# Layer 1 of a two-layer GNN with expert FFN: the expert mask moved to VectorE, the block's beginning divided

## The chip, the core and the metric

The kernel runs on one core of a Trainium2 chip. The core has five engines with their own instruction queues: TensorE (PE; its weight loads are shown apart, as PEld), VectorE (DVE), ScalarE (ACT), GpSimd (POOL) and SyncE (SP). Each engine takes its instructions in order, and an instruction waits for others by semaphores. The metric is the device time of one execution in microseconds; less is better.

## What is computed

Two layers, each a graph aggregation and then a feed-forward part, over 6250 nodes with 256 features and 100,000 edges sorted by destination. In layer 1, with which the change deals:

```python
# aggregation
h = layernorm(x) @ weight
x = x + segment_sum(edge_weight[:, None] * h[src], dst) + bias
# feed-forward part: one of 32 experts for each node
xf = layernorm(x)
idx = argmax(xf @ router_w.T + router_b, axis=-1)
h = relu(einsum('nd,ndh->nh', xf, W1[idx]) + b1[idx])          # 64 hidden values
out = relu(einsum('nh,nhd->nd', h, W2[idx]) + b2[idx])
x = x + out
```

## The kernel before

**Tiles and blocks.** The nodes are 49 tiles of 128 rows; `X` holds all of them in SBUF. The feed-forward parts work on blocks of up to 4 tiles (`NB`). `blocks1` (L360) cuts layer 1 into 13 blocks: 3 tiles, eleven times 4, and 2.

**Every expert for every node.** Layer 1 computes the hidden values of all 32 experts, 32 x 64 = 2048, in 16 chunks of 128 (`NC1`), two experts a chunk. In `hidden1` two float32 products (`k` = 0, 1) give a chunk's hidden values for the block in `ph`; a third product adds the mask. `sel[:, c, :]` (bfloat16, made once at L1025) has -2^127 (`FAR`) where a hidden row belongs to an expert, and `cold` is 1 where a node did not choose that expert, so every hidden value of an expert that was not chosen becomes hugely negative, and the ReLU on ScalarE (L989) makes it 0. `outs1` multiplies the chunk `hm` by the second weights into `py` (L1000), which gathers all 16 chunks; `end1` takes the ReLU of it, adds `X` and stores the rows.

**Which expert.** `begin1` normalises a block's rows (`norm_t`: statistics, `xn`, transposes into `nT`), multiplies by the router's weights (`pl`, L957), finds the highest expert on VectorE (L962 to L968), and transposes the one-hot rows (`pg`, L973) into `hotT` and `cold`.

**The aggregation.** `columns1` goes through the edges in columns of 128. For each column `gather` (L201) fetches 128 rows of the normalised features from DRAM by an indirect DMA that GpSimd issues; ScalarE (L230) and VectorE (L231) split the weighted rows into a float32r pair `m`; a one-hot matrix `s` (L222, VectorE, for three columns at once) sends them to their destinations in a matmul (L277) that sums in `acc`. There are 24 buffers for gathered rows, 12 for `m`. When 8 columns are done, a half tile's sums are taken out of `acc`; the steps of `summed` and `by_weight` run 2, 6 and 9 columns later (`LAG - 4`, `LAG - 1`, with `LAG` = 10), and at the last of them the sums of a tile, transposed and multiplied by the weights (L214), are added to `X` (L215). The first 64 columns are done during layer 0; 718 are left for layer 1.

**The order.** The main loop of layer 1 (L1029 to L1049) runs over blocks and chunks. Ahead of each hidden chunk and ahead of each `outs1` it calls `sums.upto`, which emits columns up to a number that `aheads` laid down: spread evenly, so that the sums of the next block are done in time for its `begin1`. That comes after chunk 11 (of 0 to 15) of the block ahead, or after chunk 13 in the first block (L1047), all in one piece. The hidden chunk `c + 1` is emitted ahead of `outs1` of chunk `c`. The compiler may shift instructions a little against this order on each engine.

Of the kernel before, what the change touches and what calls it, by code (L numbers as in the profile page):

```python
# [36 lines left out]
NC1 = NX1 * H1 // P  # L37
DST_PAD = 8192
SJ = 3
LAG = 10  # L40
EARLY = 2
FAR = -2.0 ** 127
SRC_PAD = 8191
NEAR = 576
LN_EPS = 1e-5
# [4 lines left out]
def gnn_ffn_kernel(ctx: ExitStack, tc: tile.TileContext, a, out):  # L50
# [64 lines left out]
    good1 = const.tile([P, 1], F32, name="good1")  # L115
    off = const.tile([P, 1], F32, name="off")

    which_x = const.tile([P, NX1], F32, name="which_x")
    nc.gpsimd.iota(which_x, pattern=[[1, NX1]], base=0, channel_multiplier=-1, allow_small_or_imprecise_dtypes=True)
    order = const.tile([P, NX1], F32, name="order")  # L120
    nc.gpsimd.iota(order, pattern=[[-1, NX1]], base=NX1, channel_multiplier=0, allow_small_or_imprecise_dtypes=True)
    edges_rec, edges_val = a["edges_rec"], a["edges_val"]
# [113 lines left out]
    def columns1(pool, psum, js, h, idx, w, bufs):  # L236


        hots, ahead, parts, few = bufs
        first = js.start == 0  # L240
        ends = []

        def summed(q, acc):

            yield
            if first and (q % 2 or q == 2 * NB):
                s = first_sums[:, q // 2, :]
            else:
                s = pool.tile([P, D], F32, tag="sums", name="sums", bufs=few)
            nc.scalar.activation(s, acc[:, 0, :], AF.Copy)  # L250
            nc.vector.tensor_add(s, s, acc[:, 1, :])
            halves[q] = s
            low, high = slice(0, P // 2), slice(P // 2, P)
            if q % 2:
                nc.vector.tensor_add(s[low], s[low], halves[q - 1][low])
            elif first:
                if 0 < q < 2 * NB:
                    nc.vector.tensor_add(halves[q - 1][high], halves[q - 1][high], s[high])
            else:
                if q == 2 * NB:  # L260
                    nc.vector.tensor_add(s, s, first_sums[:, NB, :])
                nc.vector.tensor_add(halves[q - 1][high], halves[q - 1][high], s[high])
                sT = pool.tile([P, 2, P], F32, tag="sT", name="sT", bufs=2)
                yield
                yield from by_weight(psum, halves[q - 1], sT, q // 2 - 1)

        for j in range(js.start, js.stop + (0 if first else LAG)):
            if j < js.stop:
                q, i = divmod(j + CS // 2, CS)
                opens = i == 0 or j == js.start  # L270
                done = i == CS - 1 or j == js.stop - 1
                if opens:
                    acc = psum.tile([P, 2, D], F32, tag="agg", name="acc", bufs=2)
                if (j - js.start) % SJ == 0:
                    s = one_hots(pool, dl_c, j, hots)
                m = weighted(pool, h, idx[:, j:j + 1], w[:, j:j + 1], ahead, parts)
                nc.tensor.matmul(acc, s[:, (j - js.start) % SJ, :], m, start=opens, stop=done)  # L277
                if done:
                    ends.append((j, summed(q, acc)))
            for at, steps in ends:  # L280
                if j - at in (0, 2, LAG - 4, LAG - 1):
                    next(steps, None)
            yield
        for _, steps in ends:
            for _ in steps:
                pass
        yield
# [69 lines left out]

    ramp = [1, 1, 2, 3] + [NB] * 9 + [3, 3]
    blocks0 = [list(range(sum(ramp[:b]), sum(ramp[:b + 1]))) for b in range(len(ramp))]
    ramp = [3] + [NB] * 11 + [2]  # L360
    blocks1 = [list(range(sum(ramp[:b]), sum(ramp[:b + 1]))) for b in range(len(ramp))]

    class Stream:
# [271 lines left out]
    with tc.tile_pool(name="layer0", bufs=1) as wp, tc.tile_pool(name="outs0", bufs=1, side="right") as wo_pool, \  # L635
# [56 lines left out]
        def aggregate0():  # L692
            for b, tiles in enumerate(blocks0):
                idx, dl, w = edges[b]
                for i, t in enumerate(tiles):
                    acc = psum.tile([P, 2, D], F32, tag="agg", name="acc", bufs=2)
                    for j in range(EW):
                        if j % SJ == 0:
                            s = one_hots(wp, dl[:, i, :], j, 3)
                        m = weighted(wp, h0, idx[:, i, j:j + 1], w[:, i, j:j + 1], 12, 6)  # L700
                        nc.tensor.matmul(acc, s[:, j % SJ, :], m, start=(j == 0), stop=(j == EW - 1))  # L701
                        if j == EW - 1:
                            for half in range(2):
                                nc.vector.tensor_add(X[:, t, :], X[:, t, :], acc[:, half, :])
                        yield

            for _ in columns1(wp, psum, range(NE), h1[:LIM, :], idx_e, w_e, (3, 12, 6, 2)):
                yield
            while True:
                yield  # L710
# [84 lines left out]
        def load1(k, half):  # L795
# [4 lines left out]
            else:  # L800
                cs = slice(half * NC1 // 2, (half + 1) * NC1 // 2)
                x = a["L1_ffn_W2"].rearrange("e h d -> (e h) d").rearrange("(c p) d -> p c d", p=P)
                nc.sync.dma_start(w2f[:, cs, :], x[:, cs, :])


        idx_e = wp.tile([P, NE], I32, name="idx_e")
        w_e = wp.tile([P, NE], F32, name="w_e")

        def early_columns():
            nc.vector.tensor_scalar(w_e, src_c[:, :NE], float(LIM), None, op0=OP.is_lt)  # L810
            nc.vector.tensor_tensor(w_e, w_e, val_c[:, :NE], OP.mult)
            nc.vector.tensor_scalar(idx_e, src_c[:, :NE], float(LIM - 1), None, op0=OP.min)


        n_late = len(late)
# [123 lines left out]

    with tc.tile_pool(name="layer1", bufs=1, reuse_waits="tile") as wp, \  # L940
            tc.tile_pool(name="psum_y1", bufs=1, space=bass.MemoryType.PSUM, reuse_waits="tile") as psum_y:

        sel_x = wp.tile([P, NX1, H1], BF, name="sel")
        sel = sel_x.rearrange("q (c s) i -> q c (s i)", s=2)
        nought = wp.tile([P, 2 * D], BF, name="nought")

        done = []
# [1 line left out]
        def begin1(pool, tiles):  # L949

            n = len(tiles)
            nw = n * P
            nT = norm_t(pool, psum, tiles)
            pl = psum.tile([P, NB, NX1], F32, tag="tr", name="pl", bufs=1)
            for j in range(n):
                for k in range(2):
# [11 lines left out]
            nc.vector.tensor_tensor(g, g, m[:, :, None].to_broadcast([P, n, NX1]), OP.is_equal)  # L968
            hots = work.tile([P, NB, P // NX1, NX1], F32, tag="hots", name="hots", bufs=1)
            nc.scalar.activation(hots[:, :n], g[:, :, None, :].to_broadcast([P, n, P // NX1, NX1]), AF.Copy)  # L970
            pg = psum.tile([P, NB * P], F32, tag="tr", name="pg", bufs=1)
            for j in range(n):
                turned = nc.tensor.transpose(pg[:, j * P:(j + 1) * P], hots[:, j], ident)  # L973
            hotT = pool.tile([P, NB * P], BF, tag="hotT", name="hotT", bufs=2)
            done[:] = [turned, nc.scalar.activation(hotT[:, :nw], pg[:, :nw], AF.Copy)]
            cold = pool.tile([P, NB * P], BF, tag="cold", name="cold", bufs=2)
            done.append(nc.vector.tensor_scalar(cold[:, :nw], pg[:, :nw], 0.5, None, op0=OP.is_lt))
            return nT, hotT, cold, nw

        def hidden1(pool, block, c):  # L980
            nT, _, cold, nw = block
            ph = psum.tile([P, NB * P], F32, tag="mm", name="ph", bufs=3)
            for k in range(2):
                nc.tensor.matmul(ph[:, :nw], w1f[:, k, c * P:(c + 1) * P], nT[:, k, :nw],  # L984
                                 start=(k == 0), stop=False)

            nc.tensor.matmul(ph[:, :nw], sel[:, c, :], cold[:, :nw], start=False, stop=True)  # L987
            hm = pool.tile([P, NB * P], F32, tag="hm", name="hm", bufs=4)
            nc.scalar.activation(hm[:, :nw], ph[:, :nw], AF.Relu, bias=b1[:, c:c + 1])  # L989
            return hm  # L990

        def outs1(block, c, now, py, n):
# [22 lines left out]
        with tc.tile_pool(name="flow1", bufs=1, reuse_waits="tile") as flow:  # L1015

            sums = Stream(columns1(flow, psum, range(NE, NREAL), h1, src_c, val_c, (5, EW + 6, 12, 4)))
            cum = [0] + [min(CS * (2 * tiles[-1] + 2) + CS // 2, NREAL) + LAG - NE for tiles in blocks1[1:]]
            plans = aheads(cum, 2 * NC1, [4] + [8] * (len(blocks1) - 1))
            block = begin1(flow, blocks1[0])  # L1020

            behind = ExitStack()
            for ins in done:
                behind.enter_context(tc.issue_after(ins.ins))
            nc.vector.tensor_scalar(sel_x, which_x[:, :, None].to_broadcast([P, NX1, H1]), 0.0, FAR,  # L1025
                                    op0=OP.is_equal, op1=OP.mult)
            nc.vector.memset(nought, 0.0)
            hm = hidden1(flow, block, 0)
            for b, tiles in enumerate(blocks1):  # L1029
# [3 lines left out]
                mine = block  # L1033
                for c in range(NC1):
                    sums.upto(plans[b][2 * c])
                    now = hm
                    if c + 1 < NC1:
                        hm = hidden1(flow, block, c + 1)
# [4 lines left out]
                    if b == 0 and c == 3:  # L1043
                        behind.close()
                    outs1(mine, c, now, py, n)

                    if c == NC1 - (3 if b == 0 else 5) and not last:  # L1047
                        after = begin1(flow, blocks1[b + 1])
                end1(flow, tiles, py)  # L1049

        with tc.tile_pool(name="slow1", bufs=1) as flow:

            def again():
                for t in range(NT):
                    block = begin1(flow, [t])
# [54 lines left out]
```

## Time and profile before

| what | us |
|---|---|
| median of 3 runs | 2898.83 (2892.92 to 2900.43) |
| profiled execution, its time | 2895.13 |
| its span | 2893.4 |
| layer 1's first gather, last gather (start) | 1828.05, 2772.42 |
| first mask matmul of blocks 1, 5, 10, 11, 12 | 1949.8, 2286.5, 2707.9, 2788.7, 2854.0 |
| last matmul's end | 2885.1 |

In the lists of groups the columns are: line, engine, operation, tiles (out<-in), shapes, count | busy time, mean duration in ns of one | idle time of the engine ahead of them and what ended it. In a list of waits: engine and line <- what it waited for: us in total, times, longest. In a timeline: start, duration, engine, line, operation, tiles, shapes, count, and in brackets the idle time ahead of it and what ended that. The slices of the whole span (40 equal ones; digits are tenths):

```profile
PE   5888848888999999999999998779999999999998
DVE  8999977778768767766566555666666666666630
POOL 4666667777767676766675527677777777777720
```

Layer 1 begins at about slice 26; all three are those of the page.

### The profile page before, as it was taken

The page shows a single profiled execution, that of the slowest core. Times are in us where ns is not written, and L with a number is a line of the kernel's source. Part 1 is how long each engine was busy: PE and PEld are TensorE (multiplying, and loading weights), DVE is VectorE, ACT ScalarE, POOL GpSimd, SP SyncE. Part 2 cuts the span into 40 slices and gives each one's busy share as a digit, 9 for nine tenths or more (in the row PEclk, how much of TensorE's full clock was granted, in tenths as well). Part 3 has the DMA queues.
Part 4 walks back from the last instruction along what each step waited for, and adds up shares of the span by engine and source line. Part 5 has one row for each costly group of instructions (what it writes and reads, how often), then busy time and mean ns, then how long its engine had stood idle before and what let it go on. Part 6 is the DMA issues. An engine that isn't in the chain of part 4 may idle for free.

```text
span 2893.4 us, 37030 instructions
## 1 busy us (share of the span) xinstructions
PE 2677.7 (93%) x10336; PEld 1750.2 (60%) x10336; DVE 2012.4 (70%) x4917; ACT 1626.1 (56%) x3790; POOL 1926.1 (67%) x1932
## 2 busy tenths in 40 slices
PE   5888848888999999999999998779999999999998
PEld 2444427665566666666666665556666666666666
DVE  8999977778768767766566555666666666666630
ACT  6777737655555555555555545455555555555532
POOL 4666667777767676766675527677777777777720
PEclk9999978999999999999999999999999999999999
DMA  4000043333333333333332214333333333333310
GB/s 150 19 19 19 19 141 97 101 100 102 92 99 95 90 101 97 91 100 96 91 102 82 78 39 135 109 108 103 107 108 109 106 108 102 108 106 109 109 44 12
DMA packets 123140, 260.73 MB, mean 90 GB/s; under 512 B 32236, under 2 KB 68904, under 8 KB 122920
## 3 DMA queue, kind: packets, MB, share of 16 engines
q0 software_dynamic: 79872, 218.21, 26.2%
q1 hardware_dynamic: 31672, 32.42, 3.4%
q10 hardware_dynamic: 11376, 7.60, 0.8%
q8 instruction: 85, 1.39, 0.2%
q14 instruction: 135, 1.11, 0.1%
HBM read 238.87 MB, written 19.25 MB: 89 GB/s over the span
## 4 chain that ended last, share of the span: by engine, by line
PE 65%; DVE 17%; DMA 8%; issue 4%; ACT 4%; POOL 1%; ACTq 0%; POOLq 0%; DVEq 0%
PE ph L748 19%; PE py L760 10%; PE py L1000 9%; PE ph L984 9%; PE acc L701 6%; PE acc L277 4%; DMA g<-h,src_c 4%; DMA g<-h,idx 3%; DVE loads L527 3%; DVE to L523 2%; DVE m L231 2%; ACT m L230 2%; PE ph L987 1%; PE ph L214 1%; POOL g L201 1%
## 5 line engine op out<-in xcount | busy, mean ns | idle before, releaser
L201 POOL DMA_INDIRECT g<-h,idx x882 | 903.1, 1024 | 391.8 <-DVE m L231 175.2
L201 POOL DMA_INDIRECT g<-h,src_c x718 | 725.6, 1011 | 227.8 <-issue 104.2
L230 ACT ACTIVATE m<-g,w 128x256 fp32r<-128x256 f32 x882 | 394.7, 500 | 260.0 <-PE acc L701 136.0
L751 ACT ACTIVATE hT<-ph,shift,scale 128x512 f32<-128x512 f32 (+3 forms) x480 | 329.0, 696 | 314.6 <-PE ph L748 313.4
L230 ACT ACTIVATE m<-g,val_c 128x256 fp32r<-128x256 f32 x718 | 349.7, 503 | 273.6 <-PE acc L277 132.2
L231 DVE SCALAR_TENSOR_TENSOR m<-g,val_c,m 128x256 fp32r<-128x256 f32 x718 | 337.1, 483 | 211.2 <-ACT m L230 207.6
L231 DVE SCALAR_TENSOR_TENSOR m<-g,w,m 128x256 fp32r<-128x256 f32 x882 | 397.7, 476 | 42.5 <-ACT m L230 41.4
L748 PE MATMUL ph<-nT,w 128*128 128x512 f32 (+3 forms) x960 | 373.1, 524 | 25.0 <-ACT hT L751 24.8
L760 PE MATMUL py<-wo,hT 128*128 128x256 f32 x1568 | 382.1, 387 | 13.8 <-DVE X L762 10.5
L1000 PE MATMUL py<-w,hm 128*128 128x256 f32 x1568 | 386.7, 385 | 3.1 <-ACT hm L989 3.1
L701 PE MATMUL acc<-m,s 128*128 128x512 f32 x882 | 341.4, 490 | 38.0 <-DVE scale L657 24.7
L984 PE MATMUL ph<-nT,w 128*128 128x512 f32 (+2 forms) x832 | 374.8, 571 | 0.0
L748 PE MATMUL ph<-hT,w 128*128 128x512 f32 (+3 forms) x960 | 368.5, 518 | 0.5 <-ACT hT L751 0.5
L760 PEld LDWEIGHTS py<-wo,hT 128*128 128x128 f32 x1568 | 294.7, 193 | 80.8 <-DVE X L762 26.9
L277 PE MATMUL acc<-m,s 128*128 128x512 f32 x782 | 332.2, 499 | 1.7 <-DVE m L231 1.7
L1000 PEld LDWEIGHTS py<-w,hm 128*128 128x128 f32 x1568 | 292.1, 193 | 52.9 <-ACT hm L989 4.6
L222 DVE TENSOR_TENSOR s<-col,dl 128x384 fp32r<-128x384 f32 x294 | 161.4, 551 | 187.0 <-PE acc L701 184.8
L748 PEld LDWEIGHTS ph<-nT,w 128*128 128x128 f32 x960 | 175.2, 195 | 174.2 <-issue 118.1
L989 ACT ACTIVATE hm<-ph,b 128x512 f32<-128x512 f32 (+2 forms) x208 | 136.8, 659 | 200.0 <-PE ph L987 199.6
L748 PEld LDWEIGHTS ph<-hT,w 128*128 128x128 f32 x960 | 176.2, 193 | 118.9 <-issue 88.3
L701 PEld LDWEIGHTS acc<-m,s 128*128 128x128 f32 x882 | 169.7, 195 | 109.8 <-issue 48.9
L984 PEld LDWEIGHTS ph<-nT,w 128*128 128x128 f32 x832 | 157.2, 191 | 101.5 <-issue 81.1
(248 smaller groups left out, 3359.0 us busy)
## 6 DMA issues: line engine op xcount, KB each, us to landing
g<-h,idx POOLq DMA_INDIRECT x882, 2.8
g<-h,src_c POOLq DMA_INDIRECT x718, 2.8
h<-hs SPq DMA_DIRECT2D x25, 256.0 KB, 2.1
X<-in_x_dram SPq DMA_DIRECT2D x12, 512.0 KB, 8.9
out_dram<-o SPq DMA_DIRECT2D x11, 512.0 KB, 3.4
h<-hs SPq DMA_DIRECT2D x9, 512.0 KB, 3.0
w<-in_L_ffn_W_dram ACTq DMA_DIRECT2D x2, 2048.0 KB, 11.2
wo<-in_L_ffn_Wo_dram ACTq DMA_DIRECT2D x1, 2048.0 KB, 20.0
```

The lines of the kernel that those rows point to most:

```text
L201: nc.gpsimd.indirect_dma_start(out=g, out_offset=None, in_=h, in_offset=bass.IndirectOffsetOnAxis(ap=idx, axis=0))
L222: nc.vector.tensor_tensor(s[:, :n], col[:, None, :].to_broadcast([P, n, P]), dl[:, j:j + n, None].to_broadcast([P, n, P]), OP.is_equal)
L230: nc.scalar.activation(m[:, 0, :], g, AF.Copy, scale=w)
L231: nc.vector.scalar_tensor_tensor(m[:, 1, :], g, w, m[:, 0, :], op0=OP.mult, op1=OP.subtract)
L277: nc.tensor.matmul(acc, s[:, (j - js.start) % SJ, :], m, start=opens, stop=done)
L701: nc.tensor.matmul(acc, s[:, j % SJ, :], m, start=(j == 0), stop=(j == EW - 1))
L748: nc.tensor.matmul(ph[:, :nw], (w1, w2)[layer][:, e, k, m * P:(m + 1) * P], src[:, k, :nw], start=(k == 0), stop=(k == 1))
L751: nc.scalar.activation(hT[:, m, :nw], ph[:, :nw], AF.Relu, bias=shift[:, layer, c:c + 1], scale=scale[:, layer, c:c + 1])
L760: nc.tensor.matmul(py, hT[:, k, j * P:(j + 1) * P], wo[:, e, k, :], start=(k == 0), stop=(k == 1))
L984: nc.tensor.matmul(ph[:, :nw], w1f[:, k, c * P:(c + 1) * P], nT[:, k, :nw], start=(k == 0), stop=False)
L989: nc.scalar.activation(hm[:, :nw], ph[:, :nw], AF.Relu, bias=b1[:, c:c + 1])
L1000: nc.tensor.matmul(py[:, j, :], now[:, cols], w2f[:, c, :], start=False, stop=(c == NC1 - 1), skip_group_check=True)
```

## The change

1. **The mask.** `sel`, `cold`, `FAR` and the mask matmul go. A bfloat16 matrix `to_expert`, made once on GpSimd, holds in row q, column (s, i) the value q - s (zero outside the first 32 rows). At the end of `begin1` one matmul of it with `hotT` gives each node's chosen expert (less s for the upper half of the rows), copied to `whose`. After the ReLU of a chunk VectorE sets to 0 what is not of the chosen expert: `hm = (whose == 2c) * hm`.
2. **The beginning in four parts.** `begin1` becomes a generator: statistics and normalised rows; transposes; router, highest expert, one-hot rows; transposes, `to_expert` and `whose`. The parts are taken at chunks 10, 11, 12 and 14 of the block ahead (12 to 15 in the first block), ahead of that chunk's work. The columns that a block needs are done with chunk 10.
3. **The columns' steps.** `LAG` is 13: a tile's sums reach `X` 12 columns after its last one, not 9.
4. **The last blocks** have 3, 2 and 1 tiles, in place of 4 and 2: 14 blocks.
5. **The early columns** write their masked weights and indices into `val_c` and `src_c` themselves.

```diff
-LAG = 10
+LAG = 13
...
-                if j - at in (0, 2, LAG - 4, LAG - 1):
+                if j - at in (0, 2, 6, LAG - 1):
...
-    ramp = [3] + [NB] * 11 + [2]
+    ramp = [3] + [NB] * 10 + [3, 2, 1]
...
+    to_expert = const.tile([P, P], BF, name="to_expert")
+    nc.gpsimd.memset(to_expert, 0.0)
+    nc.gpsimd.iota(to_expert[:NX1, :].rearrange("q (s i) -> q s i", s=2), pattern=[[-1, 2], [0, H1]], base=0,
+                   channel_multiplier=1, allow_small_or_imprecise_dtypes=True)
...
-            nT = norm_t(pool, psum, tiles)
+            mv, rstd = stats(tiles)
+            xns = []
+            for j, t in enumerate(tiles):
+                xns.append(pool.tile([P, D], F32, tag="xn", name="xn1", bufs=NB))
+                nc.vector.tensor_scalar(xns[j], X[:, t, :], mv[:, j, 0:1], rstd[:, j:j + 1],
+                                        op0=OP.subtract, op1=OP.mult)
+            yield
+            nT = pool.tile([P, 2, NB * P], F32, tag="nT", name="nT", bufs=2)
+            for j in range(n):
+                transposed(psum, xns[j], nT[:, :, j * P:(j + 1) * P])
+            yield
...
-            cold = pool.tile([P, NB * P], BF, tag="cold", name="cold", bufs=2)
-            done.append(nc.vector.tensor_scalar(cold[:, :nw], pg[:, :nw], 0.5, None, op0=OP.is_lt))
-            return nT, hotT, cold, nw
+
+            pe = psum.tile([P, NB * P], F32, tag="tr", name="pe", bufs=1)
+            nc.tensor.matmul(pe[:, :nw], to_expert, hotT[:, :nw], start=True, stop=True)
+            whose = pool.tile([P, NB * P], BF, tag="whose", name="whose", bufs=2)
+            done.append(nc.vector.tensor_copy(whose[:, :nw], pe[:, :nw]))
+            yield nT, hotT, whose, nw
...
-            nc.tensor.matmul(ph[:, :nw], sel[:, c, :], cold[:, :nw], start=False, stop=True)
             hm = pool.tile([P, NB * P], F32, tag="hm", name="hm", bufs=4)
             nc.scalar.activation(hm[:, :nw], ph[:, :nw], AF.Relu, bias=b1[:, c:c + 1])
+
+            nc.vector.scalar_tensor_tensor(hm[:, :nw], whose[:, :nw], 2.0 * c, hm[:, :nw],
+                                           op0=OP.is_equal, op1=OP.mult)
...
-            plans = aheads(cum, 2 * NC1, [4] + [8] * (len(blocks1) - 1))
-            block = begin1(flow, blocks1[0])
+            begins = [[12, 13, 14, 15]] + [[10, 11, 12, 14]] * (len(blocks1) - 1)
+            plans = aheads(cum, 2 * NC1, [2 * (NC1 - 1 - at[0]) for at in begins])
+            *_, block = begin1(flow, blocks1[0])
...
                     sums.upto(plans[b][2 * c])
+                    if c == begins[b][0] and not last:
+
+                        sums.upto(plans[b][2 * c + 1])
+                        parts = begin1(flow, blocks1[b + 1])
+                    if c in begins[b] and not last:
+                        after = next(parts)
                     now = hm
...
-                    if c == NC1 - (3 if b == 0 else 5) and not last:
-                        after = begin1(flow, blocks1[b + 1])
```

More of the change, by code (lines that the diff above doesn't have):

```diff
@@ L39 @@
 SJ = 3
-LAG = 10
+LAG = 13
 EARLY = 2
-FAR = -2.0 ** 127
 SRC_PAD = 8191
@@ L116, in gnn_ffn_kernel @@
     off = const.tile([P, 1], F32, name="off")
-    which_x = const.tile([P, NX1], F32, name="which_x")
-    nc.gpsimd.iota(which_x, pattern=[[1, NX1]], base=0, channel_multiplier=-1, allow_small_or_imprecise_dtypes=True)
+    to_expert = const.tile([P, P], BF, name="to_expert")
+    nc.gpsimd.memset(to_expert, 0.0)
+    nc.gpsimd.iota(to_expert[:NX1, :].rearrange("q (s i) -> q s i", s=2), pattern=[[-1, 2], [0, H1]], base=0,
+                   channel_multiplier=1, allow_small_or_imprecise_dtypes=True)
     order = const.tile([P, NX1], F32, name="order")
@@ L705, in aggregate0 @@
                         yield
-            for _ in columns1(wp, psum, range(NE), h1[:LIM, :], idx_e, w_e, (3, 12, 6, 2)):
+            for _ in columns1(wp, psum, range(NE), h1[:LIM, :], src_c, val_c, (3, 12, 6, 2)):
                 yield
@@ L803, in load1 @@
                 nc.sync.dma_start(w2f[:, cs, :], x[:, cs, :])
-        idx_e = wp.tile([P, NE], I32, name="idx_e")
-        w_e = wp.tile([P, NE], F32, name="w_e")
         def early_columns():
-            nc.vector.tensor_scalar(w_e, src_c[:, :NE], float(LIM), None, op0=OP.is_lt)
-            nc.vector.tensor_tensor(w_e, w_e, val_c[:, :NE], OP.mult)
-            nc.vector.tensor_scalar(idx_e, src_c[:, :NE], float(LIM - 1), None, op0=OP.min)
+            nc.vector.scalar_tensor_tensor(val_c[:, :NE], src_c[:, :NE], float(LIM), val_c[:, :NE],
+                                           op0=OP.is_lt, op1=OP.mult)
+            nc.vector.tensor_scalar(src_c[:, :NE], src_c[:, :NE], float(LIM - 1), None, op0=OP.min)
         n_late = len(late)
@@ L941, in gnn_ffn_kernel @@
             tc.tile_pool(name="psum_y1", bufs=1, space=bass.MemoryType.PSUM, reuse_waits="tile") as psum_y:
-        sel_x = wp.tile([P, NX1, H1], BF, name="sel")
-        sel = sel_x.rearrange("q (c s) i -> q c (s i)", s=2)
         nought = wp.tile([P, 2 * D], BF, name="nought")
@@ L970, in begin1 @@
             nc.scalar.activation(hots[:, :n], g[:, :, None, :].to_broadcast([P, n, P // NX1, NX1]), AF.Copy)
+            yield
             pg = psum.tile([P, NB * P], F32, tag="tr", name="pg", bufs=1)
@@ L975, in begin1 @@
             done[:] = [turned, nc.scalar.activation(hotT[:, :nw], pg[:, :nw], AF.Copy)]
-            cold = pool.tile([P, NB * P], BF, tag="cold", name="cold", bufs=2)
-            done.append(nc.vector.tensor_scalar(cold[:, :nw], pg[:, :nw], 0.5, None, op0=OP.is_lt))
-            return nT, hotT, cold, nw
+            pe = psum.tile([P, NB * P], F32, tag="tr", name="pe", bufs=1)
[3 more added lines that the diff above has]
+            yield nT, hotT, whose, nw
         def hidden1(pool, block, c):
-            nT, _, cold, nw = block
+            nT, _, whose, nw = block
             ph = psum.tile([P, NB * P], F32, tag="mm", name="ph", bufs=3)
@@ L984, in hidden1 @@
                 nc.tensor.matmul(ph[:, :nw], w1f[:, k, c * P:(c + 1) * P], nT[:, k, :nw],
-                                 start=(k == 0), stop=False)
-            nc.tensor.matmul(ph[:, :nw], sel[:, c, :], cold[:, :nw], start=False, stop=True)
+                                 start=(k == 0), stop=(k == 1))
             hm = pool.tile([P, NB * P], F32, tag="hm", name="hm", bufs=4)
             nc.scalar.activation(hm[:, :nw], ph[:, :nw], AF.Relu, bias=b1[:, c:c + 1])
+            nc.vector.scalar_tensor_tensor(hm[:, :nw], whose[:, :nw], 2.0 * c, hm[:, :nw],
+                                           op0=OP.is_equal, op1=OP.mult)
             return hm
@@ L1024, in gnn_ffn_kernel @@
                 behind.enter_context(tc.issue_after(ins.ins))
-            nc.vector.tensor_scalar(sel_x, which_x[:, :, None].to_broadcast([P, NX1, H1]), 0.0, FAR,
-                                    op0=OP.is_equal, op1=OP.mult)
             nc.vector.memset(nought, 0.0)
@@ L1054, in again @@
                 for t in range(NT):
-                    block = begin1(flow, [t])
+                    *_, block = begin1(flow, [t])
                     py = psum_y.tile([P, NB, D], F32, tag="y", name="py", bufs=1)
```

## The prediction

> **What bounds the kernel now.** I read the page first, busy shares and then the costly groups.
>
> ```profile
> PE 2677.7 (93%) x10336; PEld 1750.2 (60%) x10336; DVE 2012.4 (70%) x4917; ACT 1626.1 (56%) x3790; POOL 1926.1 (67%) x1932
> ...
> L201 POOL DMA_INDIRECT g<-h,src_c x718 | 725.6, 1011 | 227.8 <-issue 104.2
> ```
>
> TensorE looks like the bound. But the 718 gathers of layer 1 take 1.011 us each, and 227.8 / 718 = 0.32 us passes ahead of each. Next, the waits, GpSimd's alone, while layer 1 gathers (1840 to 2773 us):
>
> ```profile
> POOL g L201 <- issue: 101.1, 332, 0.3
> POOL g L201 <- DVE m L231: 52.4, 172, 0.3
> POOL g L201 <- DVE s L222: 17.1, 56, 0.3
> ```
>
> The last column is the longest wait: 0.3 us everywhere, whatever is named. GpSimd never waits for anything in layer 1; that 0.3 is its gap between two gathers. A gather each 0.946 + 0.305 + 0.06 = 1.31 us makes 64 x 1.31 = 83.9 us for a block of 4 tiles, and the middle blocks take 82.4 to 87.6 (from one block's first mask matmul to the next one's). The third view is busy time by block: blocks 9, 10 and 11.
>
> ```profile
> 2625.00:2708.00 83.00, 82.86 (x333) 56.97 (x332) 54.89 (x133) 44.85 (x101) 63.74 (x64) 1.00 0.36 108
> 2708.00:2789.00 81.00, 79.94 (x321) 54.75 (x319) 47.64 (x115) 39.78 (x86) 50.19 (x50) 1.00 0.30 90
> 2789.00:2854.00 65.00, 64.89 (x252) 43.49 (x251) 8.84 (x27) 14.24 (x26) 0.00 (x0) 1.00 0.02 9
> ```
>
> Behind the length stand PE, PEld, DVE, ACT, POOL. So the two run level: GpSimd without a pause, TensorE with some 82 us of work in a block of 84. What TensorE has to spare goes where a block begins, in waits for the normalised rows; the timeline has them at blocks 8 and 10:
>
> ```profile
> 2606.01 0.41 PE L340 MATMUL tr<-ident,xn 128*128 128x128 f32 x2 [2.89 <-DVE xn L346]
> ...
> 2772.42 0.94 POOL L201 DMA_INDIRECT g<-h,src_c  x1 [0.30 <-DVE rstd L332]
> 2772.84 0.96 DVE L346 TENSOR_SCALAR xn<-X,mv,rstd 128x256 f32<-128x256 f32 x2
> 2773.63 0.41 PE L340 MATMUL tr<-ident,xn 128*128 128x128 f32 x2 [1.05 <-DVE xn L346]
> ```
>
> The last gather is issued at 2772.4, and 120 us follow without one: TensorE alone sets that tail. The end is therefore a gate (the gathers) plus the TensorE work behind it.
>
> **The mask, TensorE's side.** Removed: 208 matmuls. One of 512 columns holds the next work back 0.21 us (in block 11 it starts at 2851.39, `py` at 2851.61), one of 256 columns 0.11 (2859.18 to 2859.29): 176 x 0.21 + 16 x 0.16 + 16 x 0.11 = 41 us. Added: one `to_expert` matmul per block, 0.054 a tile, 2.6 us in all. Ahead of the gate the saving buys nothing: a block falls to some 79 us of TensorE work and still waits for 83.9 us of gathers.
>
> **The mask, VectorE's side.** Added: 16 SCALAR_TENSOR_TENSOR of 128x512 a block; no row has that form. Its neighbours:
>
> ```profile
> L231 DVE SCALAR_TENSOR_TENSOR m<-g,val_c,m 128x256 fp32r<-128x256 f32 x442 | 207.7, 483 | 127.5 <-ACT m L230 125.1
> L222 DVE TENSOR_TENSOR s<-col,dl_c 128x384 fp32r<-128x384 f32 x147 | 81.8, 556 | 60.5 <-PE acc L277 60.4
> L977 DVE TENSOR_SCALAR cold<-pg 128x512 bf16<-128x512 f32 x7 | 4.8, 689 | 2.5 <-ACT hotT L975 2.4
> ```
>
> From 256 to 384 elements the tensor-tensor rows go from 0.42 to 0.556, 1.07 ns an element: 0.69 (L222 carried on) to 0.76 us (L231 carried on). I take 0.72: 11.5 us a block on the 55 busy now, 66 of 84. `whose` takes the place of `cold`, one copy for one. On its own this is covered: a hidden chunk has (chain of waits) 8 `py` matmuls (1.73), the next 4 `ph` (1.72) and about four columns at 0.21 (0.85) before it is read, against 0.69 for the ReLU and 0.72 for the mask.
>
> **What the masks do to the gathers.** This term decides. The timeline shows a gather growing when it begins inside a VectorE instruction that reads two operands from SBUF:
>
> ```profile
> 2763.18 0.95 POOL L201 DMA_INDIRECT g<-h,src_c  x1 [0.30 <-DMA g<-h,src_c]
> ...
> 2764.15 0.48 DVE L231 SCALAR_TENSOR_TENSOR m<-g,val_c,m 128x256 fp32r<-128x256 f32 x1 [1.15 <-ACT m L230]
> 2764.43 1.03 POOL L201 DMA_INDIRECT g<-h,src_c  x1 [0.30 <-issue]
> ...
> 2765.73 0.55 DVE L222 TENSOR_TENSOR s<-col,dl_c 128x384 fp32r<-128x384 f32 x1
> 2765.76 1.34 POOL L201 DMA_INDIRECT g<-h,src_c  x1 [0.31 <-issue]
> ```
>
> With none running 0.95; with 0.20 us of L231 left 1.03; at the start of an L222 1.34. I paired the 712 gathers from 1835 us on with what VectorE ran at their start: 261 met no such instruction and lie 0.003 us above 0.946; 309 met L231, mean +0.075; 97 met L222, mean +0.144. Where 0.24 to 0.42 us of the instruction was left, all are long, by what was left less about 0.1. Per instruction: L231 309 x 0.075 / 718 = 0.032 us; L222 97 x 0.144 / 239 = 0.058. The mask reads `whose` and `hm`, both in SBUF. Scaled by length: 0.032 x 0.72 / 0.48 = 0.048 us of gather per mask (low), 0.058 x 0.72 / 0.55 = 0.076 (from L222, nearest in length, which I take), and by what-is-left-less-0.1, 0.56 squared / 2 / 1.31 = 0.12 (high). A gain is excluded: 0.946 is what a gather takes with nothing in its way. Up to the gate at block 9's chunk 10, 9 x 16 + 10 = 154 masks: **+11.7 us** (7 to 18).
>
> The Trainium skill, "SBUF — State Buffer", section "Who interferes with whom", speaks against this change: a VectorE instruction with two SBUF inputs contends with a GpSimd one that reads SBUF, and section "SBUF: two separate sides" calls it a lock for the whole instruction. A lock throughout would make an estimated 0.72 x 0.72 / 2 / 1.31 = 0.20 us a mask, 30 us in place of the 11.7 and a time near 2928; the pairs, where short remainders cost nothing, show less.
>
> **The early, divided beginning.** Work per block is the same, only moved: statistics at chunk 10, transposes at 11, router at 12, `to_expert` at 14. It issues no DMA, and no step of it passes SP's or GpSimd's queue. But the gate moves. Before, the sums for block 10 had to be in at chunk 11 of block 9 with column 638; now at chunk 10 with column 641 (LAG 13). Three more gathers, 3 x 1.31 = 3.9, and one more chunk of TensorE work behind the gate, 3.45 + 0.85 = 4.3; less the masks of the 5 chunks left in the block, 1.1: **+7.1 us**. Against it, TensorE no longer stands at `tr L340`, since the rows have a chunk's time: 1.05 and 2.89 us in the rows shown, **-2** (0 to -4).
>
> **The work behind the gate.** From block 10's start (2707.9) to the last matmul's end (2885.1) TensorE works nearly without pause. Masks gone: 16 x 0.21 for block 10 and 16 x 6 x 0.054 for the last six tiles, -8.6; `to_expert` and one more block's fixed parts, +0.6: **-8.0**. Splitting 4+2 tiles into 3+2+1 changes no product; it lets the gate fall under block 9 rather than 10, which is in the terms above. In the last block a chunk is 0.43 + 0.43 us, against ReLU and mask of 128 elements (0.3 to 0.35 each, estimated from 0.47 at 256) with two hand-overs; 16 such steps, **+2** (0 to 4).
>
> **Costed at nothing:** `sel` (1.2 us once, VectorE), two early-column instructions against three, `to_expert`'s set-up in the start: all lie under the first gathers or loads; uncovered, under 2 us.
>
> **Sum:** 11.7 + 7.1 - 2 - 8.0 + 2 = +10.8 us. The profiled execution took 2895.1 (span 2893.4), 3.7 under the median of 2898.8; on the median this is **2910 us**. With the gather term's ends and the small ones, 2900 to 2920.
>
> **Rivals.**
> *TensorE is the bound.* Its 9s in every slice speak for it, GpSimd's waits against. Then 41 - 2.6 comes off: 2860. Chance 0.15.
> *The masks miss the gathers,* falling where a gather no longer reads: 7.1 - 2 - 8 + 2 = -1, 2898. The same comes if TensorE follows the gathers more closely: column 640 is multiplied 19.5 us after its gather, which alone needs 3.9; a lead cut by half takes off 8. Against it: the pairs. 0.16.
> *VectorE's order becomes the path* (the other side, worse than forecast). Its queue is in order, so behind a mask that waits for its ReLU stand the products L231, and a mask stands behind products that wait for gathers. The cover is 4.3 - 1.4 = 2.9 us, six L231. Past that, `py L1000` waits each step; at 0.3 us for the some 70 steps behind the gate, +20: 2930. VectorE at 80% is for it, 12 buffers of `m` against. 0.12.
> *Forecast:* 0.57.
>
> **How the numbers follow.** About 0.3%, 8.7 us, is what can be told from no change. The forecast's share splits around 2907.5: 0.35 above, 0.20 within, 0.02 faster. Rival one is faster; rival two 0.12 same, 0.04 faster; rival three slower. Faster 0.21, same 0.32, slower 0.47. The range 2876 to 2930 leaves out most of rival one and the end of rival three.
>
> **What would show it.** Right: the mean gather near 1.03 to 1.04 us with no wait over 0.3, the last one issued some 12 us later or more, L1000's waits small. Wrong: gathers still at 1.01, GpSimd waiting for buffers, or `py` waiting for VectorE.

## The result, and the profile after

The changed kernel takes 2918.7 us (median of 6 runs, 2917.4 to 2923.6), the one before beside it 2898.8: ratio 1.0073, 95% interval 1.006 to 1.0086. It is slower by some 20 us; the forecast was 2910, with 2876 to 2930 as the range. The profiled execution took 2917.4 us against 2895.1, +22.3.

The page first: its busy shares, two rows of its 40 slices, and from its list of groups the gathers (here with the 64 columns done during layer 0) and the mask. Line numbers are those of the changed kernel: the gather is L202 (L201 before), the product on VectorE L232 (L231), the one-hot rows L223 (L222), the mask L998.

```profile
PE 2655.7 (91%) x10195; PEld 1742.9 (60%) x10207; DVE 2127.3 (73%) x5148; ACT 1633.2 (56%) x3809; POOL 1951.3 (67%) x1933
...
PE   5888848889999999999999998778999999999998
POOL 4666667777766766766665527777777777777730
...
L202 POOL DMA_INDIRECT g<-h,src_c x782 | 817.9, 1046 | 297.9 <-issue 92.8
...
L998 DVE SCALAR_TENSOR_TENSOR hm<-whose,hm 128x512 f32<-128x512 bf16 (+3 forms) x224 | 140.1, 626 | 132.3 <-ACT hm L996 130.0
```

TensorE has 22 us less to do and the program is 22 us longer: TensorE's work wasn't what it was short of. VectorE has 115 us more; the mask alone keeps it busy for 140. The granted TensorE clock doesn't explain it: its mean is 0.974 before and 0.967 after, but in the stretches behind the gate, where TensorE is full, it is 1.00 in both. From 1835 us on, the group of gathers by form, and GpSimd's waits while layer 1 gathers (us in total, times, longest):

```profile
L202 POOL DMA_INDIRECT g<-h,src_c x712 | 747.1, 1049 | 216.9 <-issue 81.9 <-DVE m L232 47.8 <-DMA g<-h,src_c 18.3
```

```profile
POOL g L202 <- issue: 80.7, 265, 0.3
POOL g L202 <- DVE m L232: 47.8, 157, 0.3
...
POOL g L202 <- DVE hm L998: 8.8, 29, 0.3
```

A gather takes 1.049 us where it took 1.011, and the longest wait ahead of one is still 0.3 us, the gap. GpSimd still waits for nothing in layer 1; each of its instructions is longer. Busy time by block, from a block's first ReLU on (window, length, then PE, PEld, DVE, ACT, POOL; blocks 9, 10 and 11):

```profile
2655.00:2740.00 85.00, 78.80 (x308) 54.36 (x308) 59.82 (x137) 43.49 (x95) 66.11 (x63) 0.98 0.36 104
2740.00:2811.00 71.00, 70.95 (x281) 49.47 (x280) 48.17 (x109) 34.13 (x74) 45.57 (x44) 1.00 0.30 89
2811.00:2861.00 50.00, 49.95 (x210) 37.25 (x210) 23.00 (x56) 16.16 (x34) 0.00 (x0) 1.00 0.03 11
```

In block 9 TensorE now stands for 6 of 85 us where it was full; behind it, it is full to the end. So there is still one gate, and the difference can be cut at three marks: layer 1's first gather, the gather of column 640 (on which block 10 depends), and block 10's first ReLU. Times from the traces, in us:

| profiled run | first gather to column 640 | column 640 to block 10's first ReLU | from there to the last matmul's end |
|---|---|---|---|
| before | 843.8 | 36.9 | 176.4 |
| after | 866.4 (+22.6) | 45.8 (+8.9) | 168.6 (-7.8) |

The sum, 23.7 less the 0.5 us by which layer 1 started sooner, is the 23.2 us between the last matmuls' ends (2885.1 and 2908.3).

**Why a gather is longer.** I took each gather from 1835 us on, what it is above 0.946 us, and the VectorE instruction that ran when it began (the one begun last, where two overlap; the prediction's pairing, 309 and 97, counted a little more widely). Gathers over 1.7 us are kept apart, and small rows left out:

| running at the gather's start | before: gathers, mean excess in ns, us in all | after |
|---|---|---|
| the product `m` | 292, 78, 22.6 | 258, 104, 26.9 |
| the one-hot `s` | 96, 145, 13.9 | 96, 187, 18.0 |
| the mask | none | 67, 224, 15.0 |
| gathers over 1.7 us | 1: 4.5 us | 10: 12.3 us |
| all | 46.4 | 73.5 |

The masks' own row, 15.0 us for the 173 that ran while gathers did, is 0.087 us a mask. The other 12 us stand in rows that existed before: the same instructions cost more, and a new kind of gather has come up. The timeline shows one (start, duration, engine, instruction):

```profile
2144.77 0.69 DVE L998 SCALAR_TENSOR_TENSOR hm<-whose,hm 128x512 f32<-128x512 bf16 x1
2144.89 1.39 POOL L202 DMA_INDIRECT g<-h,src_c  x1 [0.30 <-DVE m L232]
...
2146.44 0.47 DVE L232 SCALAR_TENSOR_TENSOR m<-g,val_c,m 128x256 fp32r<-128x256 f32 x1
2146.59 2.41 POOL L202 DMA_INDIRECT g<-h,src_c  x1 [0.30 <-DVE sums L256]
2146.84 0.54 DVE L223 TENSOR_TENSOR s<-col,dl_c 128x384 fp32r<-128x384 f32 x1
2147.30 0.86 DVE L232 SCALAR_TENSOR_TENSOR m<-g,val_c,m 128x256 fp32r<-128x256 f32 x2
```

The gather at 2144.89 meets a mask with 0.57 us left and is 0.44 longer: what is left, less 0.13, as the prediction read it for single instructions. The one at 2146.59 meets a product with 0.32 us left and should cost 0.2; but the next instruction follows without a gap, and two more after it, to 2148.16. It takes 2.41 us, 1.46 more than alone: the whole row of four, 1.57 us, less 0.11. Not every gather in such a place does. Counted over layer 1, with "followed at once" for a next instruction with two SBUF operands within 0.03 us:

| met at the gather's start | before: gathers, us | after |
|---|---|---|
| no such instruction | 266, 0.9 | 244, 0.6 |
| one alone | 347, 30.0 | 267, 28.1 |
| one that is followed at once | 100, 15.4 | 200, 44.8 |

Lone instructions cost no more in all than they did: fewer meetings, and 0.105 us each against 0.086, since masks, which are longer, are among them. So the increase stands where instructions follow each other, but that doesn't mean that these gathers wait for the whole row. A gather that meets a lone instruction with 0.24 to 0.42 us left pays what is left less 0.127 us (median, in both traces). If each gather's excess is parted by that into what the first instruction explains and what was paid beyond it (over 0.06 us), the 73.5 us are 15.0 for the masks themselves, 38.9 for other first instructions (40.0 before) and 18.8 that 29 gathers paid beyond the first one (5 gathers and 5.3 us before). All 29 had begun inside a product, a one-hot row or another instruction of before; none of the 67 that met a mask paid for more than the mask. So of the 27 us, 15 are the price of the masks and 13 to 14 are longer waits in rows of other instructions.

### The profile page after: what moved, and what is told of

Read it like the earlier page. It is cut to its first block, busy times and chain, and to the rows that moved or that the text cites. A ratio compares the mean times of both kernels' runs of the same rounds, so it can differ in the third digit from the quotient of the medians.

```text
span 2915.6 us, 36965 instructions
## 1 busy us (share of the span) xinstructions
PE 2655.7 (91%) x10195; PEld 1742.9 (60%) x10207; DVE 2127.3 (73%) x5148; ACT 1633.2 (56%) x3809; POOL 1951.3 (67%) x1933
## 4 chain that ended last, share of the span: by engine, by line
PE 62%; DVE 19%; DMA 10%; ACT 4%; issue 4%; POOL 2%; ACTq 0%; POOLq 0%; DVEq 0%
PE ph L749 19%; PE py L761 10%; PE ph L993 9%; PE py L1010 8%; DMA g<-h,src_c 6%; PE acc L702 6%; PE acc L278 4%; DMA g<-h,idx 3%; DVE loads L528 3%; DVE m L232 2%; ACT m L231 2%; DVE to L524 2%; POOL g L202 1%; PE tr L341 1%; PE ph L215 1%
## 5 line engine op out<-in xcount | busy, mean ns | idle before, releaser
L202 POOL DMA_INDIRECT g<-h,idx x882 | 901.1, 1022 | 391.4 <-DVE m L232 175.4
L202 POOL DMA_INDIRECT g<-h,src_c x782 | 817.9, 1046 | 297.9 <-issue 92.8
L231 ACT ACTIVATE m<-g,val_c 128x256 fp32r<-128x256 f32 x782 | 379.1, 505 | 341.7 <-DMA g<-h,src_c 190.1
L231 ACT ACTIVATE m<-g,w 128x256 fp32r<-128x256 f32 x882 | 394.6, 500 | 256.8 <-PE acc L702 137.0
L232 DVE SCALAR_TENSOR_TENSOR m<-g,val_c,m 128x256 fp32r<-128x256 f32 x782 | 362.7, 480 | 134.3 <-ACT m L231 131.4
L232 DVE SCALAR_TENSOR_TENSOR m<-g,w,m 128x256 fp32r<-128x256 f32 x882 | 398.1, 477 | 42.6 <-ACT m L231 41.8
L749 PE MATMUL ph<-nT,w 128*128 128x512 f32 (+3 forms) x960 | 373.8, 525 | 26.9 <-ACT hT L752 26.8
L993 PE MATMUL ph<-nT,w 128*128 128x512 f32 (+3 forms) x896 | 395.6, 560 | 0.0
L278 PE MATMUL acc<-m,s 128*128 128x512 f32 x782 | 376.7, 547 | 15.5 <-DVE m L232 14.2
L702 PE MATMUL acc<-m,s 128*128 128x512 f32 x882 | 341.2, 490 | 37.9 <-DVE scale L658 24.6
L223 DVE TENSOR_TENSOR s<-col,dl 128x384 fp32r<-128x384 f32 x294 | 161.8, 552 | 186.8 <-PE acc L702 184.5
L749 PEld LDWEIGHTS ph<-nT,w 128*128 128x128 f32 x960 | 175.2, 195 | 176.7 <-issue 118.3
L996 ACT ACTIVATE hm<-ph,b 128x512 f32<-128x512 f32 (+3 forms) x224 | 140.8, 628 | 172.9 <-PE ph L993 170.0
L998 DVE SCALAR_TENSOR_TENSOR hm<-whose,hm 128x512 f32<-128x512 bf16 (+3 forms) x224 | 140.1, 626 | 132.3 <-ACT hm L996 130.0
```

The lines of the kernel that those rows point to most:

```text
L202: nc.gpsimd.indirect_dma_start(out=g, out_offset=None, in_=h, in_offset=bass.IndirectOffsetOnAxis(ap=idx, axis=0))
L223: nc.vector.tensor_tensor(s[:, :n], col[:, None, :].to_broadcast([P, n, P]), dl[:, j:j + n, None].to_broadcast([P, n, P]), OP.is_equal)
L231: nc.scalar.activation(m[:, 0, :], g, AF.Copy, scale=w)
L232: nc.vector.scalar_tensor_tensor(m[:, 1, :], g, w, m[:, 0, :], op0=OP.mult, op1=OP.subtract)
L749: nc.tensor.matmul(ph[:, :nw], (w1, w2)[layer][:, e, k, m * P:(m + 1) * P], src[:, k, :nw], start=(k == 0), stop=(k == 1))
```

## The experiments

That the second SBUF operand is the cause is so far a pairing in time. The first four kernels ran on one chip, beside 35 runs of the kernel before (2895.4 us).

**The mask reads PSUM.** The same VectorE instruction in the same place; the ReLU leaves its result in PSUM, so one operand comes from SBUF in place of two.

```diff
-            nc.scalar.activation(hm[:, :nw], ph[:, :nw], AF.Relu, bias=b1[:, c:c + 1])
+            nc.scalar.activation(ph[:, :nw], ph[:, :nw], AF.Relu, bias=b1[:, c:c + 1])
-            nc.vector.scalar_tensor_tensor(hm[:, :nw], whose[:, :nw], 2.0 * c, hm[:, :nw],
+            nc.vector.scalar_tensor_tensor(hm[:, :nw], whose[:, :nw], 2.0 * c, ph[:, :nw],
                                            op0=OP.is_equal, op1=OP.mult)
```

> The changed kernel with one thing different: the ReLU writes its chunk back into PSUM and the mask reads it there, so that each mask has one operand in SBUF in place of two; its length and its place in VectorE's queue stay. If masks cost by holding the port that GpSimd reads through: gathers of layer 1 back from a mean of 1.048 to about 1.01 us, the last one issued near 2775 us in place of 2798, and the time some 20 us under the changed kernel, 2895 to 2902 (ratio to before 0.998 to 1.001). If they cost by filling VectorE or by their place in its order: gathers may stay or fall, but the time stays at 2914 to 2922 (1.005 to 1.008).

Measured: 2901.3 us, ratio 1.0017 (1.0006 to 1.0028); the span is 2895.8, 19.8 us under that of the changed kernel (by the ratios, 1.0017 against 1.0073, it is 16 us). That is the time of the first reading; the gathers fell less than it said. The groups by form from 2200 to 2700 us, the changed kernel's first and then this one's:

```profile
L202 POOL DMA_INDIRECT g<-h,src_c x370 | 388.2, 1049 | 112.7 <-issue 41.7 <-DVE m L232 27.1 <-DMA g<-h,src_c 10.1
...
L998 DVE SCALAR_TENSOR_TENSOR hm<-whose,hm 128x512 f32<-128x512 bf16 x93 | 64.5, 694 | 29.9 <-ACT hm L996 28.7
```

```profile
L202 POOL DMA_INDIRECT g<-h,src_c x375 | 386.4, 1030 | 114.3 <-issue 42.0 <-DVE m L232 29.6 <-DMA g<-h,src_c 8.2
...
L997 DVE SCALAR_TENSOR_TENSOR hm<-whose,ph 128x512 f32<-128x512 bf16 x95 | 64.8, 682 | 33.5 <-ACT ph L996 33.2
```

The mask is as long (682 ns against 694) and VectorE as busy (2123.6 us in all against 2127.3), yet the gathers are shorter; over the whole of layer 1 1.022 us against 1.048. The excess falls from 73.5 to 54.4 us, and the 73 gathers that begin inside a mask have a mean excess of 0.0. So for the masks' own price the operand's place decides, not VectorE's time.

**The mask left out.** The mask instruction is removed, all else stays.

> The changed kernel without the mask instruction (every expert's hidden values are added, so the output is another): the whole price of the masks. Port: the same as with the mask read from PSUM within 5 us, 2890 to 2900. VectorE's time or order: clearly under that kernel, by 10 us or more, with gathers alike in both.

Measured: 2888.9 us, ratio 0.9973 (0.9962 to 0.9984). Gathers take 1.0035 us, their excess is 41.3. Neither reading had this: the time is 12 us under that with the mask out of PSUM, and the gathers are not alike. There is 13 us less excess: even a mask that costs the gathers nothing itself closes up VectorE's queue, so that products and one-hot rows stand behind each other (156 gathers meet one that is followed at once, 32.3 us, against 136 and 20.6 without a mask). That reading is of two traces; the 12 us between the medians agrees with it but may hold more.

**The two halves of the change by themselves.** First, the mask by VectorE (with `whose`, `to_expert` and the early columns) in the kernel before, the beginning in one piece; second, the changed kernel with the mask matmul on TensorE.

```diff
 (mask alone, against the kernel before)
-            nc.tensor.matmul(ph[:, :nw], sel[:, c, :], cold[:, :nw], start=False, stop=True)
             nc.scalar.activation(hm[:, :nw], ph[:, :nw], AF.Relu, bias=b1[:, c:c + 1])
+            nc.vector.scalar_tensor_tensor(hm[:, :nw], whose[:, :nw], 2.0 * c, hm[:, :nw],
+                                           op0=OP.is_equal, op1=OP.mult)
 (the rest alone, against the changed kernel: the same, the other way round)
```

> The kernel before with the mask by VectorE alone (and the early columns in place): beginning in one piece, LAG 10, last blocks of 4 and 2 as before. Port: gathers at 1.04 to 1.05 us, last one near 2795, less 8 us of mask matmuls behind the gate: 2909 to 2916 (1.0035 to 1.006). If the divided beginning is what costs, this kernel is at or under the one before: 2880 to 2900.

> The changed kernel with the mask matmul of before on TensorE: beginning in four parts, LAG 13, last blocks of 3, 2, 1. Port: gathers at 1.01 us, last one near 2773; the gate moved costs 5 to 8 us and no mask is saved behind it: 2900 to 2909 (1.0005 to 1.0035). If the divided beginning is what costs: 2912 or more.

Measured: the mask alone 2909.6 us, 1.0035 (1.0023 to 1.0048), gathers 1.0385 us; the rest alone 2897.0 us, 1.0003 (0.9992 to 1.0014), gathers 0.9987 us. The mask alone makes 10 (by the ratio) to 14 us (by the medians) of the 20; the rest alone costs nothing that can be told from no change, where 2900 us or more were expected. The three marks, for these four kernels:

| profiled run | first gather to column 640 | column 640 to block 10's first ReLU | from there to the last matmul's end |
|---|---|---|---|
| mask reads PSUM | 848.1 | 45.8 | 168.3 |
| mask left out | 838.0 | 46.0 | 167.2 |
| mask alone | 859.4 | 37.9 | 173.5 |
| rest alone | 834.4 | 43.6 | 175.9 |

The first column follows the mask and its operands (+15.6 with the mask alone, -9.4 with the rest alone). In these two traces layer 1 also starts 7 and 6 us later than in that of the kernel before, which the marks leave out. The second follows the divided beginning: 37 to 38 with it in one piece, 44 to 46 with it in four, whatever the mask does. The two halves don't add in the first column: alone they make +15.6 and -9.4, together +22.6. The gathers' excess for the rest alone is 37.8 us, under the 46.4 of before, with fewer of the lone meetings (255 for 347); why, no run tells. Parted as above (us; a rest of up to 2.9, mostly of gathers that met none of these, is left out):

| profiled run | masks themselves | other first instructions | beyond the first (gathers) |
|---|---|---|---|
| before | none | 40.0 | 5.3 (5) |
| after | 15.0 | 38.9 | 18.8 (29) |
| mask reads PSUM | 0.0 | 38.1 | 16.0 (29) |
| mask left out | none | 34.1 | 6.6 (15) |
| mask alone | 18.1 | 34.8 | 10.6 (16) |
| rest alone | none | 27.5 | 9.5 (17) |

The operand moved to PSUM takes away the first column and little else. The last one stays near its height, so it isn't the mask's second operand that makes it; it is largest with the mask and the rest together. What sets it is not shown.

**The disputed cost by itself.** The kernel before, with an idle VectorE instruction after each ReLU that nobody waits for: once with two SBUF operands, once with one, of the same length.

```diff
+            nc.vector.scalar_tensor_tensor(side[c % 2][:, :nw], cold[:, :nw], 0.0, spare[:, :nw],
+                                           op0=OP.is_equal, op1=OP.mult)
 (or, in the other kernel)
+            nc.vector.tensor_reduce(side[c % 2], spare[:, :nw], AX.X, OP.max)
```

> The kernel before with one idle VectorE instruction added per chunk, of the mask's form and length with both operands in SBUF, that reads nothing of the chunk and whose result nobody reads: the disputed price by itself, without the wait for the ReLU, the divided beginning or a saved matmul. Port: gathers at 1.035 to 1.05 us, last one at 2790 to 2800, time 15 to 25 us over the kernel before (1.005 to 1.009). If the masks cost by their place behind the ReLU: within 4 us of the kernel before (0.999 to 1.0015).

> The same with an idle VectorE instruction of about the same length that reads one operand (a maximum over 512 elements). Port: gathers stay at 1.00 to 1.02 us, time within 4 us of the kernel before (0.9985 to 1.0015). If VectorE's busy time is what counts: as slow as with two operands, within 5 us.

These two and all that follow ran on two other chips, where the kernel before takes 3279 and 3280 us and where ScalarE's product of a gathered column starts 32 to 34 us after its gather (median; 4.2 in the kernel before and 3.9 in the changed one as first measured), so only ratios on one chip are used. Measured: two operands 3329.5 us, ratio 1.0153 (1.012 to 1.0185), and 1.0091 (1.0064 to 1.0117) on the other of the two chips, the first above what was expected and the second at its upper end; one operand 3282.2, 0.9999 (0.9975 to 1.0023). By form, 2200 to 2900 us, two operands and then one:

```profile
L201 POOL DMA_INDIRECT g<-h,src_c x431 | 469.2, 1089 | 231.6 <-DVE m L231 100.5 <-issue 84.3 <-DVE hot L966 10.9
...
L992 DVE SCALAR_TENSOR_TENSOR side<-cold,spare 128x512 f32<-128x512 bf16 x96 | 62.5, 679 | 0.0
```

```profile
L201 POOL DMA_INDIRECT g<-h,src_c x447 | 453.4, 1014 | 248.1 <-DVE m L231 98.7 <-issue 96.9 <-DVE top L969 9.6
...
L992 DVE TENSOR_REDUCE side<-spare 128x1 f32<-128x512 f32 x158 | 102.1, 673 | 0.1
```

Both are 0.67 to 0.68 us long. They don't lie alike: the one with two operands reads `cold` and so comes with its block, some 15 in each 100 us; the other reads nothing of a block, and the compiler put all 208 of its instructions ahead of 2520 us, up to 56 in 100 us. That is a weaker control than was meant, though the same number of instructions, and closer together. With one operand the 71 gathers that begin inside it are 0.015 us longer on the mean; with two, the 43 are 0.327 longer (gathers over 1.7 us left out), and 39 of all gathers take over 1.7 us where there are 13 with one operand. Some 100 of its gathers meet a row of four or more, some 50 in the changed kernel: an idle instruction waits for no ReLU and stands behind others more often than a mask does.

> The idle instruction with two operands in SBUF once more, for a chip without late rows. Port: gathers at 1.035 to 1.05 us, last one at 2790 to 2800 us, 1.005 to 1.009 of the kernel before. If the masks cost by their place behind the ReLU: 0.999 to 1.0015.

**The changed kernel on the other chips.** It was run once on each of the two.

> The changed kernel once more, timed beside the runs of this call so that they share a chip: 1.006 to 1.0085 of the kernel before, as first measured.

> The changed kernel beside the others of this call. In the call before, on a chip where gathered rows landed late and GpSimd waited for buffers, all kernels took some 13% longer and this one 0.9949 of the kernel before. Where GpSimd's longest wait in layer 1 is 0.3 us again: 1.005 to 1.0085. Where rows land late: 0.993 to 0.997, since the port then costs time that GpSimd has.

Measured: 0.9949 (0.9922 to 0.9977) and 0.9928 (0.9899 to 0.9957) against the kernel before: it is faster there, and what the first text expected failed. GpSimd's waits of the first of the two while layer 1 gathers:

```profile
POOL g L202 <- DVE m L232: 162.4, 121, 12.7
POOL g L202 <- issue: 138.4, 417, 2.7
```

GpSimd waits up to 12.7 us, where it had never waited over 0.3: its 24 buffers are at times all in use. The texts above say that the rows come late, and the DMA packets of the traces don't show that. Taken 48 to a gather in order of time, a gather's last packet ends 2.4 us (median) after the gather begins, on these chips as in the first traces. What is late is the use: between 2050 and 2700 us TensorE, VectorE and ScalarE stand idle all at once for 76 and 73 us in these two traces (0.5 us in the first trace of the kernel before and 2.5 in that of the changed one). Why is not shown; the list of ScalarE's waits puts 141 us down to TensorE's `acc` and 116 to "remote", which names no engine. I read the gain as what remains of the relief of TensorE where the gathers no longer set the pace alone; that wasn't tried. Longer gathers aren't free there either: the idle instruction with two operands cost 0.9 to 1.5% on the same two chips.

**A later gate.** The mask out of PSUM with `LAG` 10 and the four parts at chunks 11, 12, 13 and 14, and, in a second version, at 12 to 15 of every block.

```diff
-LAG = 13
+LAG = 10
-            begins = [[12, 13, 14, 15]] + [[10, 11, 12, 14]] * (len(blocks1) - 1)
+            begins = [[12, 13, 14, 15]] + [[11, 12, 13, 14]] * (len(blocks1) - 1)
 (or, in the second version)
+            begins = [[12, 13, 14, 15]] * len(blocks1)
```

> The mask read from PSUM, with LAG 10 and the four parts at chunks 11 to 14 in place of 13 and 10, 11, 12, 14: the gate moved back. The prediction's term for it says 7 to 8 us less than with the mask read from PSUM alone: 0.997 to 0.9995 of the kernel before. If the early beginning hides waits of TensorE that come back: the same as that kernel or slower, 1.0015 or more.

> The mask from PSUM, LAG 10, parts at chunks 11 to 14, once more: 0.997 to 0.9995 of the kernel before by the gate's term; 1.0015 or more if the early beginning hid waits of TensorE.

> The same with the parts at chunks 12 to 15 in every block, the gate one more chunk back: by the gate's term 4 us less again, 0.996 to 0.9985. If TensorE now waits for the rows and the expert of the next block where it begins: 2 to 8 us more than with chunks 11 to 14.

Measured: chunk 11 0.9935 (0.9909 to 0.9961) and, on the other of the two chips, 0.988 (0.984 to 0.992); chunk 12 0.9868 (0.9829 to 0.9908), all against the kernel before and all under what was expected. Beside the changed kernel on the same chip (0.9949 and 0.9928) the intervals overlap, for chunk 12 by 0.001; the medians lie 9, 10 and 14 us under its medians. What of that is the mask out of PSUM and what the gate was not parted, and chunks 11 and 12 can't be told from each other. In the traces of the chip where both ran the stretch from column 640 to block 10's first ReLU is 72.8 us for the changed kernel, 68.4 at chunk 11 and 64.4 at chunk 12: about 4 us for each chunk. Whether these versions beat the kernel before where it takes 2900 us was not measured.

## Why the prediction was right, and where its sizes were off

The direction, the place and the mechanism held; the sum had +10.8 us against 22.3 measured on the profiled executions and 20 on the medians. By its terms:

**The gathers lengthened by masks, forecast +11.7 (7 to 18): measured +22.6 to the gate.** This is the term that was mis-sized, beyond its own upper end. Its price per mask was near: 0.087 us against the 0.076 taken, so 154 masks make 13.4. What failed is the step "scaled by length", which priced the masks alone and put at nothing what other VectorE instructions cost once masks stand among them: gathers kept waiting beyond the first instruction they met went from 5.3 to 18.8 us, and those over 1.7 us from 1 to 10. Per instruction, `m` went from 0.032 to 0.038 us and `s` from 0.058 to 0.075. The upper price of 0.12 was worked out with 0.56 us; its own words, 0.72 less 0.1, give 0.62 and thus 0.147 us a mask, 22.6 us in all. That this is the number measured would have been luck, since the masks' own price was 0.087. The mask's duration was right (0.694 us, forecast 0.72). That the second operand is the cause of the masks' own price is shown: with it in PSUM 73 gathers that begin inside a mask have no excess and the span is 19.8 us shorter, and an idle instruction with two operands costs 0.9 to 1.5% where one with one operand costs nothing that can be told. What raises the other 13 us stays open: with the mask out of PSUM 16.0 us were still paid beyond the first instruction.

The Trainium skill, "SBUF — State Buffer", section "Who interferes with whom", has this contention for a VectorE instruction with two SBUF inputs beside a GpSimd instruction that reads SBUF, and section "SBUF: two separate sides" a lock held for the whole instruction. The traces agree on which operands matter. On the size they differ at one end, where a gather that meets less than 0.12 us of the instruction pays nothing, and at the other, where 29 gathers waited beyond it. The estimate of 2928 that the prediction drew from the lock lay as far above the result as the forecast lay below it.

**The moved gate, +7.1, and TensorE's stalls at the transposes, -2: together +5.1, measured +8.9.** The gate's direction is shown by the four kernels' second column. For the stalls the whole change gave the wrong sign. TensorE's waits from 2200 to 2700 us, before and then after:

```profile
PE tr L340 <- DVE xn L346: 9.5, 5, 2.9
```

```profile
PE tr L341 <- DVE xn L952: 27.2, 5, 6.2
```

With the rest alone the wait is 5.6 us, under the 9.5 of before, so where TensorE keeps the mask matmul the wait with the divided beginning is shorter, as forecast (one trace each). With the mask alone, the beginning in one piece, it is 20.3; with the mask out of PSUM 23.5, without any mask 21.5. What the term left out is that a relieved TensorE comes to the rows sooner. The step "the rows have a chunk's time" also took a chunk's length for the chain from the sums to the rows. The timeline at block 9, chunk 11, shows that chain:

```profile
2711.29 0.41 DVE L216 TENSOR_TENSOR X<-X,ph 128x256 f32<-128x256 f32 x1
...
2712.65 0.42 DVE L330 BATCH_NORM_STATS2 st<-X 128x6 f32<-128x256 f32 x1
...
2714.51 0.69 DVE L998 SCALAR_TENSOR_TENSOR hm<-whose,hm 128x512 f32<-128x512 bf16 x1
...
2715.32 1.49 DVE L952 TENSOR_SCALAR xn<-X,mv,rstd 128x256 f32<-128x256 f32 x4
...
2715.90 0.66 PE L341 MATMUL tr<-ident,xn 128*128 128x128 f32 x2 [4.58 <-DVE xn L952]
```

The last sums reach `X` at 2711.3 and the rows are begun 4.0 us later, with products and a mask in VectorE's queue between. TensorE had got there 4.6 us too soon. So the wait is TensorE's spare time: the sums come with the gathers, and a TensorE with less work has more of it.

**The work behind the gate, -8.0, and the last blocks, +2: together -6.0, measured -7.8.** Right within 2 us as a sum. By halves it fits less well: that stretch shrank by 2.9 us with the mask alone and by 0.5 with the rest alone, so that the single terms came out is not shown.

**The time.** That 2918.7 us lies just inside the 2900 to 2920 of the sum is in part luck: the gather term went past its upper end, and the profiled executions differ by 22.3 us where the medians differ by 20.

**The rivals.** TensorE as the bound (2860) is out: without the mask on either engine the time falls by 6.6 us, not 38. The masks missing the gathers is out: 67 gathers began inside one and are 0.224 us longer on the mean. Its other half did happen: the lead of the gathers over their products' use by TensorE was cut (column 640 is multiplied 13.2 us after its gather, 19.5 before), but under the longer gathers no gain from it can be seen. VectorE's order as the path is out: behind the gate the stretch shrank, and `py` waits for masks for 6.6 us in all.

## What to carry to other kernels

Before giving VectorE an instruction while GpSimd issues the transfers that bound the kernel, count its SBUF operands and not only its time: one operand in PSUM made the same instruction 16 to 20 us cheaper here. Look also at what the instructions around it then cost: about half of the increase here stood in rows of others, not in the new instruction. And work taken from an engine ahead of a gate that another engine sets came back as waiting here (27.2 us in place of 9.5 between 2200 and 2700 us).

## What the runs showed of the hardware

- A gather that meets VectorE instructions with two SBUF operands back to back can wait out the whole row: 2.41 us at 2146.59 (row of four, 1.57 us left), and one of 5.45 us in the kernel before. It doesn't always: of the gathers after the change that met the first of three or more, fewer than one in ten paid for the whole row, and most paid for the first instruction alone. What decides was not found, but it goes with how far two instructions overlap. In the traces of the two kernels and of the first four experiments, of gathers that met a product with 0.13 us or more left and another such instruction at once behind it, 38 of 40 paid beyond the product where the next began 70 to 73 ns before the product's end, and 15 of 361 where it began 77 to 89 ns before. Which of the two brings about the other is open.
- An instruction with up to 0.12 us left costs the gather nothing (82 gathers after the change, mean excess 0.0); all 103 with 0.24 to 0.42 us left pay over 0.11 us, alone what is left less 0.127 (median); of the 33 that begin within 0.06 us after a product's start, 12 pay.
- A VectorE instruction of 128x512 with one operand from PSUM and one from SBUF is no slower than with both from SBUF (682 and 694 ns).
- The change's sign turned with the chip: 0.7% slower where a gathered row is used 4 us after its gather begins, 0.5 to 0.7% faster where that takes 32.
